# The last 1x1 convolution of a two-block network as seven half-size products for eight, with GpSimd forming the differences of its inputs and x1 and the results moved two blocks at a time

## The chip, the cores and the metric

The kernel runs on one core of a Trainium2 chip. The core has five engines that run side by side and meet at semaphores: TensorE (PE: matrix products, and PEld: the loads of its weights), VectorE (DVE), ScalarE (ACT), GpSimd (POOL) and SyncE (SP, which here only issues transfers). Sixteen DMA engines move data between HBM and the on-chip SBUF; transfers are issued on SP's queue and on ACT's. TensorE writes its sums into PSUM, eight banks of 512 float32 columns on each of 128 partitions, from where VectorE and ScalarE read them. All data is float32.

The metric is the device time of one launch in microseconds (us).

## The reference

Input x is 4 images of 1024 channels, 56 x 56 pixels. Two blocks follow one another; all of the first and most of the second are not touched here. What counts is the end of the second block:

```
x1  = relu(x + conv1x1(...))                  # result of the first block, 1024 channels
y2  = relu(bn(conv3x3(relu(bn(conv1x1(x1))))))  # 256 channels
out = bn(conv1x1(y2, w3, b3))                 # 1024 channels, bn over all pixels
out = relu(x1 + softplus(residual_scale) * out)
```

The batch norm of the last convolution needs the mean and variance of its result over all images. They are worked out from the mean and the second moments of y2 and from w3, so that the convolution itself can run once, with the scale (sc3) and shift (sh3) for each channel known before its results leave PSUM: out = relu(x1 + sc3 * (w3 y2) + sh3).

## The kernel before

Channels lie on the 128 partitions, so the 256 channels of y2 are two halves (KB = 2, index h) and the 1024 channels of x1 and of the result are eight tiles (KC = 8, index k). An image is cut into seven blocks (NJ = 7, index j) of 8 rows, 448 pixels (BLK). y2 of all four images stays in SBUF. x1 lies in HBM (x1_d, written by the first block) and is read again at the end.

The stages of the second block that matter here, in the order of the program:

- The winograd convolution that makes y2 ends at about 2424 us of the profiled execution. Then SP loads the filters c3w (line 1160), and after them as many x1f tiles as there are buffers (line 1325).
- Moments: ScalarE applies bn and relu to y2 in place (relu, line 1226), TensorE turns two chunks of 128 pixels (pixels, line 1196), VectorE subtracts a reference (centred, line 1210, into ytp; ref_all, line 1254, is made first), GpSimd sets one more column to 1 (line 1203), TensorE multiplies (moments, line 1215, into acc_g).
- From the moments (gram) and c3w the sums for mean and variance are formed (lines 1278 to 1319). While VectorE works on them, TensorE computes 13 tiles of the last product ahead; ScalarE stores them in SBUF (ahead, line 1275, tiles raw).
- The last product (lines 1320 to 1343). For each image n, block j and pair of channel tiles kk: SP loads the two tiles of x1 (x1f, 448 KB, pieces of 448 pixels, 1792 bytes); for each of the two k, TensorE does two products (wide, line 1165: one for each h, tile pf), VectorE computes pf * sc3 + x1 in place (line 1329), ScalarE adds sh3 and applies relu in place (line 1337); ScalarE's queue then issues the store of both tiles (line 1343; the very last two tiles are stored one by one, line 1341).

Buffers: pf takes six PSUM banks in turn (pool ps1), x1f ten SBUF buffers (pool fin). A load of x1f therefore waits until the store from the same buffer, ten loads earlier, has landed. The order of instructions on each engine is not the order of the source alone: a scheduler places them when the program is built, and semaphore waits follow from the tiles that each instruction reads and writes.

Of the kernel before, what the change touches and what calls it, by code (L numbers as in the profile page):

```python
# [8 lines left out]
F32 = mybir.dt.float32  # L9
I32 = mybir.dt.int32  # L10
AF = mybir.ActivationFunctionType
ALU = mybir.AluOpType

N, CIN, H, W = 4, 1024, 56, 56
CB = 256
KC = CIN // 128
KB = CB // 128
HW = H * W
ROWS = 8
BLK = ROWS * W  # L20
NJ = H // ROWS
# [21 lines left out]
QREST = QB - QFULL * 128  # L43
TPAD = 1
TROWS = PW * (PW - 1) + TPAD
EPS = 1e-5


# [12 lines left out]
def deform_bottleneck_then_bn_bottleneck(  # L61
# [15 lines left out]
    nc = tc.nc  # L77
# [5 lines left out]
    out_v = out.rearrange("n (k p) h w -> n p k (h w)", p=128)  # L83
# [3 lines left out]
    x1_v = x1_d.rearrange("n (k p) q -> n p k q", p=128)  # L87
# [5 lines left out]
    tables = [  # L93
        dram.tile([TROWS, 2, CB], F32, tag=f"table{n}", name=f"table{n}") for n in range(N)
    ]
# [10 lines left out]
    def cols(name, k):  # L106
        c = COLS[name]
        return ch[:, c : c + k]

    eps_t = const.tile([128, 1], F32, tag="eps", name="eps_t")  # L110
    nc.vector.memset(eps_t, EPS)
    y1_stats = const.tile([128, KB, NB * 6], F32, tag="y1_stats", name="y1_stats")
# [3 lines left out]
    def scale_shift(stats, k, g, be, name):  # L116

        mv = const.tile([128, k, 2], F32, tag=f"mv_{name}", name=f"mv_{name}")
        for i in range(k):
            nc.vector.bn_aggr(mv[:, i, :], stats[:, i])  # L120
        return scale_shift_of(mv[:, :, 0], mv[:, :, 1], k, g, be, name)

    def scale_shift_of(mean, var, k, g, be, name, bias=None):

        sc = const.tile([128, k], F32, tag=f"sc_{name}", name=f"sc_{name}")
        sh = const.tile([128, k], F32, tag=f"sh_{name}", name=f"sh_{name}")
        nc.scalar.activation(sc, var, AF.Sqrt, bias=eps_t)
        nc.vector.reciprocal(sc, sc)
        nc.vector.tensor_mul(sc, sc, g)
        if bias is None:  # L130
            nc.vector.tensor_mul(sh, mean, sc)
            nc.vector.tensor_sub(sh, be, sh)
        else:
            nc.vector.tensor_add(sh, mean, bias)
            nc.vector.tensor_sub(sh, bias, sh)
            nc.vector.tensor_mul(sh, sh, sc)
            nc.vector.tensor_add(sh, sh, be)
        return sc, sh
# [27 lines left out]
    u, first_rows = {}, []  # L166
    us = {}

    with ExitStack() as l0:
# [14 lines left out]
        ps1 = l0.enter_context(tc.tile_pool(name="ps1", bufs=2, space=bass.MemoryType.PSUM))  # L184
# [50 lines left out]
        def load_zeros():  # L235
            zero = w3p.tile([128, CB], F32, tag="s", name="zero", bufs=8)
            nc.vector.memset(zero[: PW + 2], 0.0)
            for n in range(N):
                for corner, s in enumerate((0, PW)):
                    first_row = PW - s + TPAD  # L240
                    for r0, r1 in ((0, first_row), (first_row + H * PW, TROWS)):
                        if r1 > r0:
# [49 lines left out]
        for i in range(2):  # L292
            z = psz.tile([128, 512], F32, tag="z", name=f"z_{i}")
            for c in range(4):
                nc.tensor.matmul(
                    z[:, c * 128 : (c + 1) * 128], ident, ident, start=(c == 0), stop=True,
                    skip_group_check=True,
# [544 lines left out]
    y2 = [y2p.tile([128, KB, HW], F32, tag=f"y2_{n}", name=f"y2_{n}") for n in range(N)]  # L842

    with l1:
# [8 lines left out]
        v, vs = [], []  # L853
        for p in range(6):
            t = wino.tile([128, QUADS, KB, PW], F32, tag=f"v{p}", name=f"v{p}")
# [126 lines left out]
        def bank(pool, tag, i, p, width):  # L982
            t = pool.tile([128, 512], F32, tag=tag, name=f"{tag}{p}_{i}")
            return t[:, : KB * QUADS * width].rearrange("p (o r c) -> p o r c", o=KB, c=width)
# [148 lines left out]
        for i, p in [(i, p) for i in range(len(parts)) for p in SEQ] + [(len(parts), None)]:  # L1133
            begun = begin(i, p) if p is not None else None
            if before is not None:
                j, q, _ = before
# [16 lines left out]
            before = (i, p, begun)  # L1153

    sc2, sh2 = scale_shift(y2_stats, KB, cols("g2", KB), cols("be2", KB), "bn2")
    ps2 = ctx.enter_context(tc.tile_pool(name="ps2_l1", bufs=1, space=bass.MemoryType.PSUM))
    ps1 = ctx.enter_context(tc.tile_pool(name="ps1_l1", bufs=6, space=bass.MemoryType.PSUM))
    fin = ctx.enter_context(tc.tile_pool(name="fin", bufs=10))
    c3w = fin.tile([128, KB, CIN], F32, tag="c3w", name="c3w", bufs=1)
    nc.sync.dma_start(c3w, b_w3.rearrange("(h p) o -> p h o", p=128))  # L1160

    def wide(n, j, k, name):
        pz = ps1.tile([128, BLK], F32, tag="bank", name=f"{name}_{n}_{j}_{k}")
        for h in range(KB):
            nc.tensor.matmul(  # L1165
                pz,
                c3w[:, h, k * 128 : (k + 1) * 128],
                y2[n][:, h, j * BLK : (j + 1) * BLK],
                start=(h == 0),
                stop=(h == KB - 1),  # L1170
            )
        return pz
# [14 lines left out]
    with ExitStack() as l2:  # L1187
# [47 lines left out]
        for h in range(KB):  # L1235
# [4 lines left out]
                start=True,  # L1240
                stop=True,
# [5 lines left out]
        for i in range(0, len(chunks), 2):  # L1247
            n, at, m = chunks[i + 1]
# [20 lines left out]
        raw = {}  # L1269

        def ahead(count):
            for _ in range(count):
                j, k = divmod(len(raw), KC)
                t = stat.tile([128, BLK], F32, tag=f"raw{j}_{k}", name=f"raw_{j}_{k}")
                nc.scalar.copy(t, wide(0, j, k, "pa"))
                raw[0, j, k] = t

        ahead(1)
        mirror = ps1.tile([128, 512], F32, tag="bank", name="mirror")
        nc.tensor.transpose(mirror[:, :128], gram[:, 0, 1], ident)  # L1280
        nc.vector.tensor_copy(gram[:, 1, 0], mirror[:, :128])
# [33 lines left out]
    sc3, sh3 = scale_shift_of(  # L1315
        mom[:, 0], mom[:, 2], KC, cols("g3", KC), cols("be3", KC), "bn3", bias=cols("b3", KC)
    )
    nc.vector.tensor_scalar_mul(sc3, sc3, sp)
    nc.vector.tensor_scalar_mul(sh3, sh3, sp)
    for n in range(N):  # L1320
        for j in range(NJ):
            blk = slice(j * BLK, (j + 1) * BLK)
            for kk in range(0, KC, 2):
                x1t = fin.tile([128, 2, BLK], F32, tag="x1f", name=f"x1f_{n}_{j}_{kk}")
                nc.sync.dma_start(x1t, x1_v[n, :, kk : kk + 2, blk])
                last = (n, j, kk) == (N - 1, NJ - 1, KC - 2)
                for d in range(2):
                    k = kk + d
                    nc.vector.scalar_tensor_tensor(  # L1329
                        x1t[:, d, :],  # L1330
                        raw.pop((n, j, k), None) or wide(n, j, k, "pf"),
                        sc3[:, k : k + 1],
                        x1t[:, d, :],
                        ALU.mult,
                        ALU.add,
                    )
                    nc.scalar.activation(  # L1337
                        x1t[:, d, :], x1t[:, d, :], AF.Relu, bias=sh3[:, k : k + 1]
                    )
                    if last:  # L1340
                        nc.scalar.dma_start(out_v[n, :, k, blk], x1t[:, d, :])
                if not last:
                    nc.scalar.dma_start(out_v[n, :, kk : kk + 2, blk], x1t)


# [51 lines left out]
```

## Time and profile before

Three runs took 2872.01, 2874.92 and 2883.12 us; the median is 2874.92. The profiled execution took 2878.01 us, of which its span, from first to last instruction, is 2876.2.

| stretch of the span, us | what runs | TensorE busy | DMA, GB/s |
|---|---|---|---|
| 2100 to 2400 | winograd convolution | 291 of 300 | 17 to 75 (by 100 us) |
| 2450 to 2550 | moments, sums, 13 tiles ahead | 100 of 100 | 1 |
| 2600 to 2800 | last product | 200 of 200 | 304 to 307 |
| 2862 to 2876.2 | end of the last product, last stores | until 2871.8 | |

How to read what follows: a group row gives line, engine, operation, output<-inputs, shape and count, then busy us and mean ns of one, then the engine's idle time just ahead of these instructions and what ended it. A float32 product appears as two MATMUL instructions. Rows of matmuls overlap one another, so their spacing is read from a stretch of them and not from one row's duration. Busy shares are averages over stages with different limits; a stage's limit is read from that stage alone. Transfers on SP's queue are q1, on ACT's q10.

The last three steps of the span, from the timeline: VectorE's last addition runs from 2871.84 for 0.68 us, the last relu from 2872.56 for 0.67, and the last store is issued at 2873.26.

### The profile page before, as it was taken

The page shows a single profiled execution, that of the slowest core. Times are in us where ns is not written, and L with a number is a line of the kernel's source. Part 1 is how long each engine was busy: PE and PEld are TensorE (multiplying, and loading weights), DVE is VectorE, ACT ScalarE, POOL GpSimd, SP SyncE. Part 2 cuts the span into 40 slices and gives each one's busy share as a digit, 9 for nine tenths or more (in the row PEclk, how much of TensorE's full clock was granted, in tenths as well). Part 3 has the DMA queues.
Part 4 walks back from the last instruction along what each step waited for, and adds up shares of the span by engine and source line. Part 5 has one row for each costly group of instructions (what it writes and reads, how often), then busy time and mean ns, then how long its engine had stood idle before and what let it go on. Part 6 is the DMA issues. An engine that isn't in the chain of part 4 may idle for free.

```text
span 2876.2 us, 39294 instructions
## 1 busy us (share of the span) xinstructions
PE 2774.1 (96%) x12001; PEld 1922.0 (67%) x12001; DVE 2067.4 (72%) x4961; ACT 1497.7 (52%) x3069; POOL 1152.1 (40%) x998
## 2 busy tenths in 40 slices
PE   9988999999999999999999989999989998999999
PEld 4455566767666676677676657666779998955554
DVE  2286778788787788777788898878669886344444
ACT  2254564565555555555565656666644554234444
POOL 0165656576655456656555575554400000000000
PEclk9999999999999999999999999999999999999999
DMA  8698898999999998999999989999721102059997
GB/s 277 199 367 301 323 349 310 328 317 339 356 323 336 346 310 314 335 331 352 331 342 291 361 304 350 359 328 340 233 100 47 47 23 79 1 187 307 308 302 265
DMA packets 337109, 792.17 MB, mean 275 GB/s; under 512 B 33240, under 2 KB 183296, under 8 KB 336896
## 3 DMA queue, kind: packets, MB, share of 16 engines
q0 software_dynamic: 127296, 462.48, 45.1%
q1 hardware_dynamic: 179120, 275.78, 28.7%
q10 hardware_dynamic: 30480, 51.39, 4.8%
q8 instruction: 95, 1.56, 0.2%
q14 instruction: 118, 0.97, 0.1%
HBM read 640.68 MB, written 143.48 MB: 273 GB/s over the span
## 4 chain that ended last, share of the span: by engine, by line
PE 84%; DMA 6%; DVE 4%; ACT 3%; issue 2%; SPq 1%; another core or an unknown queue 0%; POOL 0%; ACTq 0%; DVEq 0%; POOLq 0%
PE acc L544 18%; PE pf L1165 11%; PE acc L626 11%; PE pr L600 11%; PE acc L316 10%; PE q L992 7%; PE stp L516 6%; DMA g<-table,idxs 5%; PE acc_g L1215 2%; PE pm L395 2%; DVE s L491 2%; PE b L992 2%; PE tp L1196 1%; PE pa L1165 1%; PE ftp L369 1%
## 5 line engine op out<-in xcount | busy, mean ns | idle before, releaser
L479 POOL DMA_INDIRECT g<-table,idxs x900 | 1141.5, 1268 | 918.7 <-DVE s L491 252.6
L491 DVE SCALAR_TENSOR_TENSOR s<-g,wts,s 128x256 f32<-128x256 f32 (+1 forms) x2700 | 1169.5, 476 | 332.4 <-ACT s L489 190.1
L544 PE MATMUL acc<-sts,w 128*128 128x256 f32 (+2 forms) x3528 | 723.1, 355 | 4.9 <-ACT sts L522 3.9
L544 PEld LDWEIGHTS acc<-sts,w 128*128 128x128 f32 x3528 | 601.7, 190 | 53.9 <-ACT sts L522 5.7
L489 ACT ACTIVATE s<-g,wts 128x256 f32<-128x256 f32 x900 | 425.0, 511 | 251.4 <-DMA g<-table,idxs 109.7
L600 PE MATMUL pr<-r,w 128*128 128x512 f32 (+2 forms) x896 | 368.7, 550 | 16.7 <-ACT pr L596 9.5
L626 PE MATMUL acc<-x1t,c1w 128*128 128x512 f32 (+2 forms) x896 | 361.7, 546 | 17.0 <-issue 10.9
L316 PE MATMUL acc<-xt,w 128*128 128x448 f32 x896 | 357.9, 543 | 8.5 <-DMA xt<-in_x_dram 7.5
L1165 PE MATMUL pf<-y,c3w 128*128 128x448 f32 x844 | 317.4, 539 | 0.0
L516 PEld LDWEIGHTS stp<-ident,s 128*128 128x128 f32 (+1 forms) x1800 | 211.3, 141 | 140.6 <-issue 91.3
L600 PEld LDWEIGHTS pr<-r,w 128*128 128x128 f32 x896 | 165.8, 192 | 164.3 <-issue 92.6
L626 PEld LDWEIGHTS acc<-x1t,c1w 128*128 128x128 f32 x896 | 169.0, 192 | 159.1 <-issue 106.0
L1329 DVE SCALAR_TENSOR_TENSOR x1f<-pf,sc_bn,x1f 128x448 f32<-128x448 f32 x211 | 144.2, 683 | 172.5 <-PE pf L1165 155.8
L516 PE MATMUL stp<-ident,s 128*128 128x128 f32 (+1 forms) x1800 | 253.2, 273 | 14.7 <-DVE s L491 10.3
L1165 PEld LDWEIGHTS pf<-y,c3w 128*128 128x128 f32 x844 | 160.4, 190 | 156.8 <-issue 118.4
L316 PEld LDWEIGHTS acc<-xt,w 128*128 128x128 f32 x896 | 166.6, 191 | 147.0 <-issue 141.9
L522 ACT COPY sts<-stp 128x512 f32<-128x512 f32 (+2 forms) x504 | 242.6, 530 | 17.6 <-PE stp L516 15.2
L1337 ACT ACTIVATE x1f<-x1f,sh_bn 128x448 f32<-128x448 f32 x224 | 148.3, 667 | 173.7 <-DVE x1f L1329 173.7
L611 ACT ACTIVATE x1t<-pr,ch 128x512 f32<-128x512 f32 (+2 forms) x224 | 142.0, 634 | 156.5 <-PE pr L600 136.7
L636 ACT COPY y<-acc 128x512 f32<-128x512 f32 (+2 forms) x112 | 59.5, 531 | 209.0 <-PE acc L626 193.6
L526 DVE TENSOR_TENSOR sts<-sts 128x512 f32<-128x512 f32 (+2 forms) x252 | 155.1, 615 | 0.7
L596 ACT COPY pr<-xr 128x512 f32<-128x512 f32 (+2 forms) x224 | 121.4, 542 | 4.1
(221 smaller groups left out, 2383.2 us busy)
## 6 DMA issues: line engine op xcount, KB each, us to landing
xt<-in_x_dram SPq DMA_DIRECT2D x112, 448.0 KB
x1f<-x_d SPq DMA_DIRECT2D x112, 448.0 KB
out_dram<-x1f ACTq DMA_DIRECT2D x111, 448.0 KB
xr<-in_x_dram SPq DMA_DIRECT2D x128, 256.0 KB
x_d<-x1t SPq DMA_DIRECT2D x128, 256.0 KB
table<-ft SPq DMA_DIRECT2D x56, 384.0 KB
g<-table,idxs POOLq DMA_INDIRECT x900
xr<-in_x_dram SPq DMA_DIRECT2D x64, 192.0 KB
```

What stands on the lines that cost most here:

```text
L316: nc.tensor.matmul(acc, w1[:, k, h * 128 : (h + 1) * 128], xts[n, j, k - k % 2][:, k % 2, :], start=start, stop=(k == KC - 1), skip_group_ ...
L479: nc.gpsimd.indirect_dma_start(out=g[:m], out_offset=None, in_=tables[n].rearrange("r q c -> r (q c)"), in_offset=bass.IndirectOffsetOnAxi ...
L489: nc.scalar.activation(s[:m], g[:m, 0:CB], AF.Copy, scale=wt[:, 0])
L491: nc.vector.scalar_tensor_tensor(s[:m], g[:m, corner * CB : (corner + 1) * CB], wt[:, corner], s[:m], ALU.mult, ALU.add,)
L516: nc.tensor.transpose(banks[h][:, t * 128 : t * 128 + m], s[:m, h * 128 : (h + 1) * 128], ident[:m, :m],)
L522: nc.scalar.copy(to, banks[h][:, :size].rearrange("p (e q) -> p e q", e=2))
L526: nc.vector.tensor_sub(sts[:, 5:7, :half], sts[:, 1:4:2, :half], sts[:, 0:2, :half])
L544: nc.tensor.matmul(sums[i], w2[:, a, k], sts[:, b, :half], start=(k == 0 and i % 2 == 0), stop=(k == TAPS - 1), skip_group_check=True,)
L600: nc.tensor.matmul(z, w3[:, h, k * 128 : (k + 1) * 128], r2[:, h, :size], start=False, stop=(h == KB - 1), skip_group_check=True,)
L626: nc.tensor.matmul(z, c1w[:, k, h * 128 : (h + 1) * 128], x1ts[k], start=False, stop=(i == KC // 2 - 1), skip_group_check=True,)
L992: nc.tensor.matmul(ps[:, o].rearrange("p r c -> p (r c)"), wt, x, start=first and j == 0 and (alone or o == 0), stop=last and j == len(pai ...
L1165: nc.tensor.matmul(pz, c3w[:, h, k * 128 : (k + 1) * 128], y2[n][:, h, j * BLK : (j + 1) * BLK], start=(h == 0), stop=(h == KB - 1),)
```

## The change

The blocks of an image are taken in couples: blocks 0 and 1, 2 and 3, 4 and 5 of one image, and block 6 of image 0 with block 6 of image 1 (of image 2 with that of image 3). That makes 14 couples (twos). A couple has four input tiles, two halves of channels for each of its two blocks: b11, b21 of the first and b12, b22 of the second. Two channel tiles of the result, k and k + 1 (low and high), for both blocks are four tiles of results. Their filters are four 128 x 128 squares (a(e, h), e for low or high, h for the half of y2's channels). So a couple and two channel tiles are a product of 2 x 2 by 2 x 2 squares, and it is done with seven products for eight (the Winograd form of Strassen's scheme).

- Four sums of filters for each pair of channel tiles (c3s) are made once, by VectorE, in sums_of_filters.
- Four differences of inputs for each couple (t) are made by GpSimd in sums_of_input, one couple ahead, in two buffers.
- The first couple, blocks 0 and 1 of image 0, is still done directly: 13 of its 16 tiles are the ones computed ahead (raw).
- The other 13 couples with 4 pairs of channel tiles are 52 objects Pair. Each has three PSUM banks, c11, u and v, of which there are two sets (pool psf, opened after the pools of the stages before are closed). The shared product a(0,0) b11 goes to c11, and ScalarE copies it to u (the first two pairs compute it twice instead). u then collects three more products, and is read after each of them; v collects two and is read after each; c11 one more. Each reading is an addition of u, v or c11, times sc3, to the x1 tile. So there are six additions for a pair.
- The seven products of one pair are interleaved with those of the pair before.
- x1f tiles hold one channel tile of two blocks, 128 x 896, in place of two channel tiles of one block: the same size. There are 12 buffers for 10. Where the blocks are neighbours one transfer has pieces of 3584 bytes; for the couples of blocks 6 there are two transfers of 1792-byte pieces. One relu covers 896 columns. The last tile is stored in one transfer.

```diff
+FIN = 12
...
-    fin = ctx.enter_context(tc.tile_pool(name="fin", bufs=10))
+    fin = ctx.enter_context(tc.tile_pool(name="fin", bufs=FIN))
...
+    def sums_of_filters():
+        nc.vector.tensor_add(c3s[:, 0], quarter[:, 1, 0], quarter[:, 1, 1])
+        nc.vector.tensor_sub(c3s[:, 1], c3s[:, 0], quarter[:, 0, 0])
+        nc.vector.tensor_sub(c3s[:, 2], quarter[:, 0, 0], quarter[:, 1, 0])
+        nc.vector.tensor_sub(c3s[:, 3], quarter[:, 0, 1], c3s[:, 1])
...
         ahead(1)
+        sums_of_filters()
...
+    def load_x1(two, k):
+        t = fin.tile([128, 2 * BLK], F32, tag="x1f", name=f"x1f_{two[0][0]}_{two[0][1]}_{k}")
+        move(nc.sync.dma_start, k, two, t, False)
+        return t
+
+    def add(t, k, e, ps):
+        to = t[:, e * BLK : (e + 1) * BLK]
+        nc.vector.scalar_tensor_tensor(to, ps, sc3[:, k : k + 1], to, ALU.mult, ALU.add)
+
+    def finish(t, k, two):
+        nc.scalar.activation(t, t, AF.Relu, bias=sh3[:, k : k + 1])
+        move(nc.scalar.dma_start, k, two, t, True)
...
+        sub = nc.gpsimd.tensor_sub
+        sub(t[:, 0], b12, b11)
+        sub(t[:, 1], b22, t[:, 0])
+        sub(t[:, 2], b22, b12)
+        sub(t[:, 3], b21, t[:, 1])
...
+    l3.close()
+
+    psf = ctx.enter_context(tc.tile_pool(name="psf", bufs=2, space=bass.MemoryType.PSUM))
...
+        def p1(self):
+            self.c11, self.u, self.v = (self.bank(tag) for tag in ("c11", "u", "v"))
+            self.product(self.c11, self.a(0, 0), self.b11, True, False)
+            if self.i < 2:
+                self.product(self.u, self.a(0, 0), self.b11, True, False)
+            else:
+                nc.scalar.copy(self.u, self.c11)
+
+        def p2(self):
+            self.product(self.c11, self.a(0, 1), self.b21, False, True)
+            add(self.low, self.k, 0, self.c11)
+
+        def p5(self):
+            self.product(self.v, self.s(0), self.t[:, 0], True, False)
+            add(self.high, self.k + 1, 1, self.v)
+
+        def p6(self):
+            self.product(self.u, self.s(1), self.t[:, 1], False, False)
+            add(self.low, self.k, 1, self.u)
+
+        def p3(self):
+            self.product(self.v, self.s(3), self.b22, False, True)
+            add(self.low, self.k, 1, self.v)
+
+        def p7(self):
+            self.product(self.u, self.s(2), self.t[:, 2], False, False)
+            add(self.high, self.k + 1, 1, self.u)
+
+        def p4(self):
+            self.product(self.u, self.a(1, 1), self.t[:, 3], False, True)
+            add(self.high, self.k + 1, 0, self.u)
```

In the built program the order of the instructions before the last product is the old one on TensorE, VectorE, ScalarE and SP, but for two transposes that change places and for the four sums of filters. Those stand on VectorE right after ref_all, ahead of and between the first three subtractions into ytp. From the third pair or so on, TensorE's order repeats every seven products: p5 of a pair, p1 of the next, p2 and p6 of the pair, p4 of the one before, p3 and p7 of the pair. On ScalarE the relu of a high tile is followed by the copy to u for the pair two later, and then by the store of that high tile.

## What I expect

> **What bounds the kernel now.** I read the page's chain of waits first, then its groups of instructions, then the stage itself in the views of windows and of the chain in order of time. The change touches one stage, the last product (line 1165, tile pf), so the question is what ends last there. From the page:
>
> ```profile
> PE 2774.1 (96%) x12001; PEld 1922.0 (67%) x12001; DVE 2067.4 (72%) x4961; ACT 1497.7 (52%) x3069; POOL 1152.1 (40%) x998
> ...
> L1165 PE MATMUL pf<-y,c3w 128*128 128x448 f32 x844 | 317.4, 539 | 0.0
> ...
> L1329 DVE SCALAR_TENSOR_TENSOR x1f<-pf,sc_bn,x1f 128x448 f32<-128x448 f32 x211 | 144.2, 683 | 172.5 <-PE pf L1165 155.8
> ...
> L1337 ACT ACTIVATE x1f<-x1f,sh_bn 128x448 f32<-128x448 f32 x224 | 148.3, 667 | 173.7 <-DVE x1f L1329 173.7
> ```
>
> TensorE idles 0.0 us before its 844 pieces; VectorE and ScalarE idle about as long as they work, waiting for TensorE in turn. The chain in order of time ends with one unbroken piece, and a window from the middle gives the other engines and the DMA:
>
> ```profile
> 2554.60 317.22 PE pf L1165 x844
> ```
>
> ```profile
> 2700.00:2750.00 50.00, 50.00 (x135) 25.28 (x134) 22.55 (x33) 22.41 (x34) 0.00 (x0) 1.00 0.96 311
> ```
>
> The columns after the window's length are busy us of PE, PEld, DVE, ACT, POOL, then the clock granted, the DMA's busy share and GB/s. TensorE is full at clock 1.00, GpSimd does nothing, the DMA looks nearly full. 844 pieces are 211 tiles x 2 halves of channels x 2 pieces: one product of 448 columns takes 2 x 317.22/844 = 0.752 us (the 539 ns of a row overlap their neighbours), a tile 1.50, eight products 6.01.
>
> **The change, part by part.**
>
> *Products removed.* Two blocks by two tiles of output channels were 8 products and are 7. The 14 couples of blocks less the first are 13, with 4 couples of channel tiles each: 52 pairs. The first couple keeps its 13 stored tiles and 3 direct ones. So 211 x 2 = 422 products become 3 x 2 + 52 x 7 + 2 (the first two pairs do the shared product twice) = 372. **50 x 0.752 = 37.6 us** come off a path that has nothing beside it. A pair takes 7 x 0.752 = 5.26 us if TensorE stays full.
>
> *VectorE.* 6 additions a pair for 4: 6 x 0.683 = 4.10 of 5.26 us, 78%, one behind each product but the shared one. In the order of the built program, a product that writes on an accumulator again comes at least two products (1.50 us) after the one whose addition it waits for; the addition is done 0.04 + 0.16 (a piece's row runs 539 ns, its slot 376) + 0.68 = 0.88 us after its product. Hidden, by 0.6 us.
>
> *ScalarE.* A pair has two relus of 896 columns (448 take 0.667, 784 at line 1103 0.945, so 0.83 ns a column: 1.04 us), two issues of stores (0.38 each in the timeline) and a new copy of the shared product from one PSUM bank to another (no such row: PSUM to SBUF at line 1275 took 0.53, SBUF to PSUM at line 596 0.49 and 0.60 for 384 and 512 columns; I take 0.54, with 0.45 and 0.65 as ends). 3.4 of 5.26 us. But the copy stands behind the relu of the high tile, and the next pair's accumulation waits for it: **the tightest new wait**. Behind the waiting matmul stand all of TensorE's products. From the end of the slot of the product p4: addition 0.88, relu dispatched 0.04 later and 0.93 to the copy's start (two relus in a row start 0.56 us apart in the timeline, not 0.67), copy 0.54, some 0.1 back: 2.5 us, against four products, 3.0. Cost 0, 0.5 us to spare; if the estimate is 0.8 short, 0.3 x 52 = 16 us.
>
> *GpSimd's differences.* 4 subtractions of 448 columns a couple, 52 in all, while the couple takes 21 us; the first 8 run after the last memset at line 1203, 35 us before they are needed. GpSimd has no row with two inputs here: memsets of 2 and 112 columns took 102 and 193 ns, 0.82 ns a column for one stream, so three streams give 1.2 us at most and one 0.47. The Trainium skill (GPSIMD Engine Reference, Performance versus the Vector engine) has 4497 ns for 2048 columns, so by estimate 1.0 us. About 4 of 21 us, and hidden in all of these. The same page speaks against the change: elementwise work belongs on VectorE, being twice as fast there. Here VectorE would need 0.56 us per difference (392 columns took 0.556 in line 954's row, 448 some 0.61), pushing it to 4.7 of 5.26 us; GpSimd is idle, so following the rule would buy nothing. A second rule there and in SBUF — State Buffer, Who interferes with whom, decides more: a VectorE instruction with two SBUF inputs and a GpSimd one that reads SBUF shut each other out, whole instructions long. The additions read one operand from PSUM, so by the rule they do not contend: cost 0. Only the stored tiles' additions do, at 2547 to 2556, and by then GpSimd is through. The trace can't confirm it, as GpSimd does no reading in it. If they did contend, each difference could hold an addition for 1.0 us with 0.5 to spare: 0.5 x 52 = 26 us.
>
> *Loads and stores.* 1.835 MB a pair (four tiles in, four out) in 5.26 us is 349 GB/s, for 305 now. The share 0.96 says that there is no room. Another stretch says there is: when the first buffers came free the queues were both full:
>
> ```profile
> DMA packets 2395, 4.05 MB, mean 405 GB/s; under 512 B 142, under 2 KB 2394, under 8 KB 2394
> ...
> q10 hardware_dynamic: 1287, 2.17, 56.3%
> q1 hardware_dynamic: 1107, 1.87, 48.6%
> ```
>
> That is 2565 to 2575 us, stores and loads half and half, at 405 GB/s with the same 1792-byte pieces (401 in the next 10 us). So the share counts open packets, not work. The Trainium skill (DMA: Bandwidth & Descriptors, Where 436 GB/s comes from) says that HBM gives a core some 358 GB/s; by it a pair needs 5.13 us, still under 5.26, with 0.13 to spare; by the trace 4.5. The measurement decides: cost 0. If the share were right, 305/0.955 = 320 GB/s, a pair took 5.74 and 24.5 us were lost. The pieces double to 3584 bytes in 12 of 14 couples, which I count as nothing. Buffers: 12 for 10 of the same size; 62 loads were issued by 2700 us against 54 used, a lead of some 22 us; a tile is now held longer (the high one by two pairs), leaving about 17 of 31.6 us. The waits on SP and on ACT's store issues are for transfers four loads or stores earlier, 10 us.
>
> *Sums of filters.* Four VectorE operations of 512 columns (682 ns at line 526). The built program puts them between ref_all and the first three ytp of the moments, not where the source has them. ytp waited until 2430.28 anyway; the first sum runs 2429.84 to 2430.52, so 0.25 us late; the other three fall before 2434.53, where VectorE idled 2.71. The first needs c3w, landed about 2428 by SP's wait. Cost **0.25**, ends 0 and 1.5.
>
> *Start of the stage.* The new PSUM pool's first product waits for VectorE and ScalarE to leave the old banks: last direct tile's addition, 0.9 us plus 0.1. Cost **1.0**, ends 0 and 2.5.
>
> *End.* The last product must wait for the addition before it (1.0), the last relu is of 896 columns (+0.37), the last store is 448 KB, not 224 (229 KB at 400 GB/s: +0.57). Cost **1.9**, ends 1 and 3.
>
> **Sum.** 37.6 - 0.25 - 1.0 - 1.9 = 34.4 us. The profiled execution took 2878.0 (span 2876.2); less 34.4 that is 2843.6. It lay 3.1 over the median of the three runs, 2874.9; from the median 2840.5. I forecast 2841, 1.2% faster.
>
> **The rivals.**
> - *The DMA becomes the bound* at what its share suggests, 320 GB/s: gain 34.4 - 24.5 = 10, 2865. For it: 0.96, and 58% of SP's queue time for no more bytes. Against: 405 GB/s for 20 us. 9%.
> - *A wait between engines sets the pair*, the copy behind the relu 0.3 us late: gain 18, 2857. For it: 0.5 us is what I have to spare over five hand-overs. Against: each has a row. 9%.
> - *GpSimd's lock makes it slower.* If additions and differences do shut each other out, a difference's length decides: beyond 0.5 + 34.4/52 = 1.16 us of hold per difference the gain is gone. Held 1.5 us: 52 x 1.0 = 52 us lost, 2892. For it: no row shows the two engines reading together. Against: the rule exempts operands in PSUM, and my price is 1.0. 5%.
> - *It does not do what it says*: the scheduler's order leaves TensorE gaps at each change of couple, say 1 us x 12: 2853, inside the range. 7%.
>
> **How the numbers follow.** My case, all covers hold, has 70%: its own range is 2836 to 2847 (the run's spread of 3 and the ends of the three small costs). To leave out no more than 2 in 10 it reaches to the copy's case: 2835 to 2859. A measurement tells 0.5%, 14.4 us, from nothing: faster means under 2860.5. That is my case, the order's gaps and most of the copy's case, 70 + 7 + 9 less a tail of 1, so 0.85; same is the DMA's case and that tail, 0.10; slower the lock's, 0.05.
>
> **What would show it.** Right: c11, u and v rows with 732 pieces and next to no idle time, a pair each 5.26 us in the stage's windows, clock 1.00, GB/s near 349, the last load row unwaited for. Wrong: PE idle before the second c11 piece released by ACT (copy); DVE idle released by x1f's load, with GB/s stuck near 320 (DMA); additions longer than 0.69 us wherever POOL is busy (lock).

## The result, and the profile after

Six runs of the changed kernel took 2829.93 to 2847.63 us, median 2845.73, beside 2874.43 for six of the kernel before: ratio 0.989, with a 95% interval from 0.9865 to 0.9916. The forecast was 2841, in a range of 2835 to 2859. The profiled execution took 2845.98, its span 2844.2: **32.0 us less than the span before, where the sum of the prediction had 34.4.**

From the page, the busy line:

```profile
PE 2740.3 (96%) x11901; PEld 1903.5 (67%) x11901; DVE 2141.3 (75%) x5069; ACT 1487.6 (52%) x3007; POOL 1216.8 (43%) x1050
```

100 MATMULs fewer, which is 50 products; 108 VectorE instructions more (104 additions, 4 sums of filters), 52 on GpSimd. TensorE's share is 96% as before: less work, and still the bound. Groups of the changed kernel (the idle time ahead of them stands behind the second bar):

```profile
L1360 ACT ACTIVATE x1f<-x1f,sh_bn 128x896 f32<-128x896 f32 x112 | 116.0, 1041 | 150.4 <-DVE x1f L1357 121.8
...
L1357 DVE SCALAR_TENSOR_TENSOR x1f<-u,sc_bn,x1f 128x448 f32<-128x448 f32 x156 | 106.6, 684 | 18.9 <-PE u L1409 9.4
...
L1409 PE MATMUL c<-y,c3w 128*128 128x448 f32 x208 | 88.9, 540 | 2.3 <-ACT u L1424 1.4 <-DVE x1f L1357 0.9
...
L1424 ACT COPY u<-c 128x448 f32<-128x448 f32 x50 | 26.2, 525 | 0.8 <-ACT x1f L1360 0.8
...
L1381 POOL TENSOR_TENSOR t<-y 128x448 f32<-128x448 f32 x13 | 14.8, 1139 | 0.0
```

The prices that the trace of before did not have: the copy from bank to bank 0.525 us (taken as 0.54), the relu of 896 columns 1.041 (1.04), a difference on GpSimd 1.14 (1.0, between 0.47 and 1.2). TensorE's only waits in the whole stage, in the view of waits (us in total, times, longest):

```profile
PE c L1409 <- ACT u L1424: 1.4, 1, 1.4
PE c L1409 <- DVE x1f L1357: 0.9, 1, 0.9
PE u L1409 <- DVE x1f L1357: 0.8, 1, 0.8
```

The two on VectorE are the start and the end of the stage, both in the prediction. The first, on ScalarE's copy, is not. The view of windows says where it lies (busy us of PE, PEld, DVE, ACT, POOL, then clock, DMA share, GB/s):

```profile
2560.00:2600.00 40.00, 39.66 (x106) 20.03 (x106) 27.57 (x42) 17.29 (x21) 4.46 (x4) 1.00 0.97 355
2600.00:2640.00 40.00, 38.58 (x103) 19.19 (x102) 29.40 (x45) 18.17 (x22) 8.92 (x8) 1.00 0.95 325
2640.00:2800.00 160.00, 160.00 (x427) 80.94 (x426) 125.05 (x184) 75.47 (x91) 32.06 (x29) 1.00 0.99 349
```

From 2640 to 2800 TensorE is full and the DMA moves the 349 GB/s that the prediction worked out. 1.42 us are missing before that. The chain in order of time leaves TensorE just there:

```profile
2606.26 5.97 DMA out_dram<-x1f
2612.28 4.80 DMA x1f<-x_d
2617.11 5.62 DMA out_dram<-x1f
2622.86 5.71 DMA x1f<-x_d
2634.53 1.50 PE u L1409 x4
```

Loads and stores hold the chain in turn. In the built program transfers of both kinds take eight semaphores in rotation, and an issue waits until the transfer eight issues before it has landed: a store may so wait for a load. At 2628.57 the last of these loads lands, and only then ScalarE, which had finished its copy at 2626.06, issues the store it stood before; it is 2.5 us behind. How that reaches TensorE is seen in the timeline of those microseconds (start, length, what; in brackets the idle time and its releaser; ACTq is ScalarE's issuing of transfers):

```profile
2629.66 1.04 ACT L1360 ACTIVATE x1f<-x1f,sh_bn 128x896 f32<-128x896 f32 x1 [3.60 <-DVE x1f L1357]
...
2630.73 1.21 ACTq L1346 DMA_DIRECT2D out_dram<-x1f  x2
...
2631.18 0.91 PE L1409 MATMUL c<-y,c3w 128*128 128x448 f32 x2
...
2631.99 1.04 ACT L1360 ACTIVATE x1f<-x1f,sh_bn 128x896 f32<-128x896 f32 x1 [1.29 <-DVE x1f L1357]
...
2632.93 0.53 ACT L1424 COPY u<-c 128x448 f32<-128x448 f32 x1
...
2633.51 1.02 PE L1409 MATMUL c<-y,c3w 128*128 128x448 f32 x2 [1.42 <-ACT u L1424]
...
2634.37 0.92 PE L1409 MATMUL u<-t,c3s 128*128 128x448 f32 x2
```

Here a couple of blocks 6 is stored, so a tile is two issues ("x2"). They take ScalarE another 1.21 us, where one issue in the steady stretch takes 0.34. The relu of the high tile stands behind them, the copy behind the relu, and the second product into c11 behind the copy. The loss is more than the 1.42 listed: from the row of c at 2631.18 to that of u at 2634.37 are 3.19 us for two products, which need 1.50. So 1.69.

### The profile page after: what moved, and what is told of

It reads as the page before. It is cut to its first block, busy times and chain, and to the rows that moved or that the text cites. A ratio compares the mean times of both kernels' runs of the same rounds, so it can differ in the third digit from the quotient of the medians.

```text
span 2844.2 us, 39220 instructions
## 1 busy us (share of the span) xinstructions
PE 2740.3 (96%) x11901; PEld 1903.5 (67%) x11901; DVE 2141.3 (75%) x5069; ACT 1487.6 (52%) x3007; POOL 1216.8 (43%) x1050
## 4 chain that ended last, share of the span: by engine, by line
PE 82%; DMA 8%; DVE 3%; ACT 3%; issue 2%; SPq 1%; another core or an unknown queue 1%; POOL 0%; ACTq 0%; POOLq 0%; DVEq 0%
PE acc L545 19%; PE pr L601 11%; PE acc L627 11%; PE acc L317 10%; PE q L993 8%; PE stp L517 6%; DMA g<-table,idxs 5%; PE u L1409 4%; PE c L1409 2%; PE v L1409 2%; PE acc_g L1227 2%; PE pm L396 2%; PE b L993 2%; DVE s L492 2%; PE tp L1208 1%
## 5 line engine op out<-in xcount | busy, mean ns | idle before, releaser
L1360 ACT ACTIVATE x1f<-x1f,sh_bn 128x896 f32<-128x896 f32 x112 | 116.0, 1041 | 150.4 <-DVE x1f L1357 121.8
L1357 DVE SCALAR_TENSOR_TENSOR x1f<-u,sc_bn,x1f 128x448 f32<-128x448 f32 x156 | 106.6, 684 | 18.9 <-PE u L1409 9.4
L993 PE MATMUL q<-v,u 128*128 128x196 f32 x576 | 109.6, 337 | 9.9 <-DVE v L945 8.7
L525 DVE TENSOR_TENSOR sts<-sts 128x256 f32<-128x256 f32 (+2 forms) x252 | 97.4, 387 | 25.4 <-ACT sts L523 21.3
```

The lines of the kernel that those rows point to most:

```text
L993: nc.tensor.matmul(ps[:, o].rearrange("p r c -> p (r c)"), wt, x, start=first and j == 0 and (alone or o == 0), stop=last and j == len(pai ...
```

## The experiments

Chips and executions differ by 10 us and more ahead of the stage in question, so the ratio is always to runs of the kernel before on the same chip. For effects under 0.2% I compare a second number, read from each profile: **the length of the stage**, from the first direct product's row (pf) to the end of the span. It was 321.8 us before and 289.4 after. The changed kernel run again on another chip (after_again, at the end) gave 289.7, and the last kernel below 286.7 and 286.6 in its two executions. Every other length is that of one execution.

**1. Eight products again.**

```diff
-            if self.i < 2:
+            if self.i < len(pairs):
```

> Every pair computes the shared product twice, as the first two pairs do, and copies nothing: 8 products a pair, 50 more in all, the rest of the change as it is (pieces of two blocks, differences by GpSimd, six additions). Theory (the stage costs what its products cost, 0.752 us each): span 2844.2 + 50 x 0.752 - 2.0 for the waits on the copy, which go = 2880, a pair 6.01 us, the ratio to the kernel before 1.000 to 1.004. Rival (a part of the gain comes from the larger transfers): a span under 2870, ratio under 0.998. Rival (the additions or the DMA set the pair already, just under 5.26 us): no different from the theory here, since both have more room at 6.01 us.

Ratio 1.0012 (1.0000 to 1.0023), span 2866.8, stage 324.9. The stage grew by 35.5; the theory had 37.6 - 2.0 = 35.6. The 2880 was worked out on the other chip's span, the ratio and the stage are free of that. All that the change brought is gone with its 50 products, although pieces, buffers, GpSimd's differences and six additions stay (the 50 copies to u go, since the second product takes their place). A window of it (columns as above):

```profile
2640.00:2800.00 160.00, 160.00 (x427) 80.94 (x426) 109.53 (x161) 52.56 (x54) 31.20 (x28) 1.00 0.90 306
```

TensorE just as full, the DMA at 306 GB/s.

**2. The transfers in pieces of two blocks alone.** The loop of the first couple for all couples; no sums, no differences:

```diff
+    for two in twos:
+        for k in range(KC):
+            t = load_x1(two, k)
+            for e, (n, j) in enumerate(two):
+                add(t, k, e, raw.pop((n, j, k), None) or wide(n, j, k, "pf"))
+            finish(t, k, two)
```

> The part of the change that moves x1 and the results in pieces of two blocks, by couples of blocks, alone: all couples by eight direct products, no sums of filters, no differences. Theory (transfers hidden before and after): the kernel before plus what the longer last relu and store add, about 1 us: 2876, ratio 0.999 to 1.002. Rival (the larger pieces give part of the gain): 2865 or less, ratio under 0.997.

Ratio 1.0006 (0.9995 to 1.0018). Its chain has the same piece as the kernel before, to the hundredth:

```profile
2539.95 317.22 PE pf L1177 x844
...
2857.91 1.04 ACT x1f L1359
```

The stage took 322.7, 0.9 more than before: the longer last relu and store. The theory holds; larger pieces are worth nothing by themselves.

**3. All transfers split, and 4. none split into two issues.** The third kernel moves every tile in two issues; the fourth moves the two couples of blocks 6 in one issue each, with their small pieces as they are:

```diff
     def neighbours(two):
-        return n == m and i == j + 1
+        return False
```

```diff
+        if m == n + 1:
+            view = (out_v if store else x1_v)[n : n + 2, :, k, blk].rearrange("n p b -> p n b")
+            issue(view, of) if store else issue(of, view)
+            return
```

> Seven products as in the changed kernel, but every transfer of a tile split into two of one block (1792-byte pieces, twice the issues on SP and ScalarE). Prediction's step (size of pieces counted as nothing): 2846, ratio 0.990, TensorE idle as in the changed kernel. Theory (a split transfer is two issues, so that the wait for the store four issues earlier is a wait for two tiles instead of four, and ScalarE's copy then comes late): TensorE idle 1 us or more a couple, released by the copy, 2855 to 2862. Rival (DMA cannot hold 349 GB/s with small pieces, 320 at most): pairs of 5.74 us, 2870, and TensorE waits wherever x1 is late.

> The transfers of the two couples made of the last blocks of two images (split into two issues in the changed kernel) as one issue each, with the same 1792-byte pieces. Theory (the number of issues sets how far ahead ScalarE can store): no TensorE idle time released by the copy at 2630 (1.7 us with its effects), span 2842.3, time 2844. Rival (the small pieces themselves are slow there): the idle time stays near 1.4 us, span 2844.

All split: ratio 0.9891 (0.9872 to 0.9911), stage 293.1, which is 3.7 more than the changed kernel. All of TensorE's waits on the copy, from the timeline:

```profile
2580.08 1.02 PE L1409 MATMUL c<-y,c3w 128*128 128x448 f32 x2 [0.73 <-ACT u L1424]
...
2586.71 1.02 PE L1409 MATMUL c<-y,c3w 128*128 128x448 f32 x2 [1.75 <-ACT u L1424]
...
2597.37 1.02 PE L1409 MATMUL c<-y,c3w 128*128 128x448 f32 x2 [0.55 <-ACT u L1424]
...
2603.62 1.02 PE L1409 MATMUL c<-y,c3w 128*128 128x448 f32 x2 [0.72 <-ACT u L1424]
```

and its window afterwards:

```profile
2640.00:2800.00 160.00, 160.00 (x427) 80.85 (x426) 124.39 (x182) 76.54 (x91) 33.51 (x31) 1.00 1.00 348
```

The theory of a wait in every couple fell: there are four waits, all within 66 us of the stage's start (2537.4), and then none. The prediction's step, by which nothing should have changed, is off by the 3.7 us as well. The rival of the DMA fell too: 348 GB/s with nothing but 1792-byte pieces, at a share of 1.00.

One issue each: ratio 0.9877 (0.9856 to 0.9898), stage 288.1, 1.3 less than the changed kernel. TensorE begins its last product 281.3 us into the stage, for 283.0 in the changed kernel; that is the whole 1.69. From there to the end of the span, with the last addition, relu and store, it is 6.8 us for 6.4. Its windows over the place of the wait:

```profile
2560.00:2600.00 40.00, 40.00 (x108) 20.00 (x107) 30.67 (x47) 18.31 (x22) 8.92 (x8) 1.00 0.96 341
2600.00:2640.00 40.00, 40.00 (x108) 20.30 (x107) 31.54 (x47) 19.45 (x24) 8.95 (x8) 1.00 0.98 348
```

No idle time, with the same bytes in the same pieces. So **the number of issues makes the wait, not the size of the pieces**. How much of that is the shorter way back to the transfer waited for, and how much ScalarE's longer issuing, the run does not separate. For the first speaks that with two issues a tile eight issues are one pair's transfers, 5.26 us, while loads and stores in the chain above took up to 5.97. But it makes a wait only within the first 80 us of the stage: the second couple of blocks 6, stored from 2760 to 2784 with two issues of 0.82 to 1.00 us a tile, has none. That transfers land later at first because the first couple's tiles, most of them computed ahead, are stored nearly at once is argued, not shown: no run spread those stores out.

**5. The differences on VectorE** (GpSimd does none of them then):

```diff
-        sub = nc.gpsimd.tensor_sub
+        sub = nc.vector.tensor_sub
```

> The changed kernel with its differences of the input computed by VectorE in place of GpSimd. Prediction's step (following the rule buys nothing; VectorE at 4.7 of 5.26 us): ratio to the kernel before as for the changed kernel, 0.987 to 0.990, a difference 0.61 us. Theory with a cost (four differences at once hold up the additions behind them by up to 2.4 us, with 0.6 us to spare, so TensorE waits 1 to 2 us in each of 11 couples): TensorE idle 11 to 22 us released by VectorE, ratio 0.993 to 0.996. Rival (GpSimd's differences do hold up VectorE unseen): ratio lower than 0.987.

Ratio 0.9912 (0.9889 to 0.9935), stage 299.3: 9.9 more than the changed kernel. The waits of TensorE in its stage:

```profile
PE v L1409 <- DVE x1f L1357: 4.2, 9, 0.5
PE u L1409 <- DVE x1f L1357: 1.8, 2, 1.1
PE c L1409 <- ACT u L1424: 1.4, 2, 0.9
PE c L1409 <- DVE x1f L1357: 0.9, 1, 0.9
```

A difference takes 0.62 us there, half of GpSimd's 1.14, and VectorE has room for it in the mean. But four of them come between the additions of one pair, and nine times a product on v is late for it. The theory with a cost was right in kind but not in size: VectorE releases 6.9 us of idle time here, of which 1.7 stand in the changed kernel too, so 5.2 are new, for its 11 to 22. The stage loses more than is listed, because a wait costs more spacing than its row says (see the last section). The timed ratio lies between the ranges of the two expectations and could not tell this kernel from the changed one; the stage's length can. Ahead of the stage this kernel is 1.2 us shorter (127.6 us from ScalarE's row for the scale of y2's bn to the first pf row, for 128.8), where two groups of transposes stand in another order, so that 8.7 of the 9.9 reach the whole.

**6. Each difference four times over**, on GpSimd:

```diff
         sub(t[:, 3], b21, t[:, 1])
+        for _ in range(3):
+            sub(t[:, 0], b12, b11)
+            sub(t[:, 1], b22, t[:, 0])
+            sub(t[:, 2], b22, b12)
+            sub(t[:, 3], b21, t[:, 1])
```

> The changed kernel with every difference of the input computed four times over by GpSimd: 16 operations of 1.14 us a couple, 18.2 of its 21.05 us. Prediction's step (hidden, and no holding up between the two engines where an addition reads PSUM): additions stay at 0.684 us with GpSimd busy beside them, ratio 0.987 to 0.991, span within 2 us of the changed kernel's stage. Rival (each difference holds an addition for its own length, 0.5 us hidden): at least 12 x 16 x 0.6 = 115 us more, ratio over 1.02, and additions over 1 us long.

Ratio 0.9915 (0.9893 to 0.9938), stage 297.5. In the steady stretch, and for the durations of the additions (ns, min/median/max):

```profile
2640.00:2720.00 80.00, 80.00 (x214) 40.47 (x213) 62.56 (x92) 37.72 (x45) 65.58 (x60) 1.00 0.98 356
```

```profile
L1357 DVE SCALAR_TENSOR_TENSOR x1f<-u,sc_bn,x1f x156: 673/684/685, 2558.0 to 2832.9; 128x448 f32<-128x448 f32 x156
```

GpSimd is busy for 82% of the time, TensorE is full, and no addition, those of v and c11 included, takes longer than 0.686 us. The rival, that each difference holds an addition up, is gone. Yet the stage is 8.1 us longer, where the prediction's step allowed 2, and 7.7 of that are lost at its start. Ahead of it VectorE works out sc3 and sh3 in tiny operations of 8 columns, while GpSimd now runs 32 differences in a row. From the timeline of this kernel:

```profile
2532.04 5.81 DVE L1325 TENSOR_TENSOR mom<-mom 128x8 f32<-128x8 f32 x1
...
2532.32 1.15 POOL L1386 TENSOR_TENSOR t<-y 128x448 f32<-128x448 f32 x1
...
2536.66 1.16 POOL L1385 TENSOR_TENSOR t<-y,t 128x448 f32<-128x448 f32 x1
...
2537.90 1.14 POOL L1387 TENSOR_TENSOR t<-y,t 128x448 f32<-128x448 f32 x1
2537.97 1.10 DVE L136 TENSOR_TENSOR sh_bn<-ch,sh_bn 128x8 f32<-128x8 f32 x1
...
2542.52 7.23 DVE L1357 SCALAR_TENSOR_TENSOR x1f<-raw,sc_bn,x1f 128x448 f32<-128x448 f32 x12
```

and the same operation in the changed kernel, where GpSimd has finished its eight differences by then:

```profile
2546.09 0.17 DVE L1325 TENSOR_TENSOR mom<-mom 128x8 f32<-128x8 f32 x1
```

5.81 us for 0.17: the operation squares mom and reads both inputs from SBUF, and it ends only when the fifth difference that began after it ends. A later one of its kind (L136) takes 1.10 us, until one difference has ended. So the rule in the Trainium skill (SBUF — State Buffer, Who interferes with whom) agrees with both halves of this run: operations with two SBUF inputs were shut out, additions with one input from PSUM were not. From the square of mom to the first stored tile's addition it is 10.5 us, for 1.9 in the changed kernel. What waits for sc3 follows: in the view of waits TensorE stands 2.6 us before a direct product, for the banks of the tiles ahead, and 4.0 before the first c11 (0.9 in the changed kernel).

That is 5.7 us more, as listed. Most of the rest of the loss at the start is TensorE's clock, the column behind POOL:

```profile
2552.00:2554.00 2.00, 1.74 (x3) 0.97 (x4) 0.12 (x1) 1.66 (x2) 0.00 (x0) 0.62 0.96 341
2554.00:2556.00 2.00, 2.00 (x4) 0.77 (x4) 0.00 (x0) 1.92 (x2) 0.00 (x0) 0.52 0.93 281
```

Behind the two waits it was granted at 0.62 and 0.52 of full speed, and the first three products of the pairs are 1.41, 1.49 and 1.13 us apart, for 0.83, 0.75 and 0.75 in the changed kernel, whose clock is at 1.00 there. That is 1.7 us.

**7. Eight buffers for twelve.**

```diff
-FIN = 12
+FIN = 8
```

> The changed kernel with 8 buffers for x1 and the results in place of 12. Prediction's step on buffers: 12 give a lead of some 17 us; 4 fewer take 10.5 us of it, and 6.5 us are left, about what one transfer of 448 KB takes (5 to 6 us in the chain). Theory: VectorE waits for x1 and TensorE for VectorE, 0.3 to 1 us a pair after the start: 2855 to 2890. Rival (the lead is still enough): ratio 0.987 to 0.991, as with 12.

Ratio 0.9908 (0.9885 to 0.9931), stage 297.0: 7.6 more than with 12. VectorE's first row of waits:

```profile
DVE x1f L1357 <- DMA x1f<-x_d: 29.5, 20, 3.8
```

x1 comes late 20 times in 52 pairs, and TensorE's waits add up to 6.2 us, for 3.1 in the changed kernel. The theory has the kind of the loss, at less than half of its lowest price (0.3 us a pair would be 16). The ratio lies in the rival's range; it is the stage and the waits for x1 that speak against the rival.

**8. A kernel that takes back what was lost at the ends.** One issue for the couples of blocks 6; the accumulators in the old ring of six banks; the last tile's relu and store in halves:

```diff
-            t = psf.tile([128, 512], F32, tag=tag, name=f"{tag}_{self.i}")
+            t = ps1.tile([128, 512], F32, tag="bank", name=f"{tag}_{self.i}")
...
+    now.p7()
+    now.p3()
+    finish(now.low, now.k, now.two)
+    half(now.high, 1)
+    now.p4()
+    half(now.high, 0)
```

> The changed kernel with the transfers of the two couples of last blocks in one issue each; the products' accumulators in the ring of six banks that the direct products used, so that the first does not wait for a new pool; and the last tile finished and stored in halves, the first half while TensorE computes the last product. Theory: against one issue each alone, 0.9 us less at the start and 0.9 us less at the end: from the first direct product to the end of the span 288.0 - 1.8 = 286.2 us, ratio 0.987. Rival (the ring's order puts a pair's second product on an accumulator closer to the copy, and TensorE waits for the copy in every pair): 20 us more, ratio 0.994.

Ratio 0.9883 (0.9862 to 0.9903), stage 286.7 for 286.2. The end came as expected: from TensorE's last row to the end of the span 4.8 us, with one issue each alone 5.8, in the changed kernel 5.4. The start did not: the first c11 no longer waits for a bank, but the scheduler now puts two products on one u next to each other in the first pairs, and the view of waits has that one (at 2559) and the one at the end:

```profile
PE u L1413 <- DVE x1f L1364: 1.6, 2, 0.8
```

The rival's wait in every pair, 20 us in all, did not come. To see both kernels side by side they ran once more on one chip:

> The changed kernel, unaltered, on the same chip as the kernel below. Ratio 0.989, between 0.987 and 0.991. From the first direct product to the end of the span 289.4 us, of which 2 us are TensorE's waits on the copy 70 to 80 us into the stage, if the cause (too many stores at the start of the stage, and split transfers right after them) is in the program; 287.4 if they were a chance of the one execution.

> The kernel with one issue for each transfer, the ring of banks and the last tile in halves, once more beside the changed kernel: 286.7 us from the first direct product to the end of the span, 2.7 less than the changed kernel, ratio to the changed kernel 0.999, which is less than the timed rounds can tell from 1.

The changed kernel: ratio 0.9895 (0.9870 to 0.9920), stage 289.7, again with one wait of 1.4 us on the copy, so it is in the program and no chance. The other: 0.9873 (0.9851 to 0.9895), stage 286.6. The stage is 3 us shorter in both executions; the intervals of the ratios overlap, so in the timed runs the gain is not shown.

## Why the prediction was right

| step | predicted, us | measured, us | read from |
|---|---|---|---|
| 50 products less | -37.6 | -37.6 | a pair each 5.26 in the chain; experiment 1 |
| ahead of the bn and relu of y2 | 0 | +0.6 | its scale row (ACT sc_bn) 2425.44, now 2426.02 |
| sums of filters | +0.25 | -0.2 | from that row to the first pf row 129.00, now 128.78 |
| start of the stage | +1.0 | +1.1 | row of u at 2561.17, 0.75 for c, six pf products from 2554.80 |
| copy late | 0 | +2.1 | 1.69 at 2633.5, 0.3 on the copy at 2833.0, 0.1 without visible cause at 2600.3 |
| last product's wait | +1.0 | +1.0 | last u at 2837.80, its row 1.02 long |
| last relu and store | +0.94 | +1.0 | last TensorE row to end of span 4.4, now 5.4 |
| sum | -34.4 | -32.0 | span 2876.2, now 2844.2 |

*The bound and the products*: right. Both halves of it were tried: the products back, in place of the copies, gave the old time; the transfers alone gave nothing.

*Sums of filters*: the cost of 0.25 did not show. The first product into acc_g comes 0.1 us later behind the scale row, but the second group of them 0.2 sooner, two transposes having changed places; from there the lead stays. The 0.6 us ahead of that row lie where the two programs do the same, and are what two executions differ by. It is luck that this difference is so small: the executions here begin the stage between 2536.8 and 2561.1 us. The stage itself, free of that, is 32.4 us shorter.

*VectorE hidden with 0.6 us to spare*: right. It is 78% busy from 2640 to 2800, and TensorE waits for it at the two ends only. Experiment 5 shows how near the edge that is.

*ScalarE's copy*: right for the steady pair. There a copy ends at 2827.68, and the product that waits for it has its slot at 2828.30. At the end of the stage a copy ends 0.14 us behind such a slot (2832.95 for 2832.81) and 0.30 are lost; so a copy must end some 0.16 ahead of the slot, and the steady pair has about 0.46 us to spare, for a forecast 0.5. Wrong at two places. At that end the last pair has no next pair's first product in front of the one that waits, which the prediction did not count: 0.3 us. The other is the larger, and the step that failed there is the cost of 0 with "0.5 us to spare", together with the sentence that the waits on ACT's store issues are for transfers four loads or stores earlier, 10 us. In a couple of blocks 6 a tile is two issues, so that is two tiles and half that time. The prediction counted two issues of stores a pair and 0.38 us each everywhere, though the diff has four in these couples. With 1.7 us there, 0.3 at the end and 0.1 without visible cause the term was 2.1 us for 0.

*GpSimd hidden, no lock*: right, and the price of 1.14 for 1.0 was of no account. To follow the page and leave the elementwise work to VectorE would not merely have bought nothing, as the prediction said, but lengthened the stage by 9.9 us.

*The DMA*: right. 349 GB/s were carried at a share of 0.99, and 348 at 1.00 in small pieces, where the kernel before had 305 at 0.96 and experiment 1 has 306 at 0.90. The share is no measure of room. Piece size at nothing was right as well.

*Buffers*: the lead of some 17 us was enough, and with four buffers less it was not.

*From the profiled execution to the median*: the sum was 2.4 under the profiled execution, 2843.6 for 2845.98, which is the copy's 2.1 and the small terms. The forecast took a further 3.1 off, because the first profiled execution lay over its median; the changed kernel's profiled execution lies on its median. Most of the 4.7 us between forecast and median are these two.

## What to carry to other kernels

Where a stretch shows one engine full with no idle time, count that engine's instructions, and price the rest only by whether it stays covered. For every wait that is covered by a margin, look for the place where the margin is smallest: the transfers with more issues, the start of the stage, a burst of work on the covering engine. An engine with room in the mean can still be the wrong place for four operations at once. GpSimd, busy for 82% of the time, ran beside VectorE's additions at no cost, since these read one input from PSUM. Keep it away from a chain of tiny operations that read both inputs from SBUF: one of them stood for 5.81 us.

## What the hardware showed beyond that

- A VectorE operation that is shut out need not get its turn after one GpSimd instruction: the 8 columns of experiment 6 stood while five more differences began and ended, 5.81 us. It is one case. Three later operations of 8 columns in the same run took 0.98, 1.10 and 1.16 us, about one difference each, and more differences followed the one that let the first through. Why that one had to wait for five is open.
- TensorE's clock came down behind a standstill of 2.6 and another of 4.0 us with two products between them (experiment 6: 0.62, then 0.52, at 1.00 again from 2556). Behind waits of 1.75 us with all transfers split and of 2.2 us with eight buffers it was 1.00. So the price of a wait can grow with its length; where between these lengths it begins, no run here shows.
- A wait of TensorE costs more than its row says: 1.69 us of spacing for 1.42 listed. The row ahead of the wait is drawn 0.16 us past its slot, and the pair of rows after it is 1.02 long for 0.92; together that is the 0.27 missing.
